# Cross-attention with hand-written order tables: two of three tables rewritten

## The chip, the cores and the metric

The kernel runs on one core of a Trainium2 chip. The metric is the time of one execution on the device in microseconds (us), as the median of several runs. A core has five engines that run side by side: TensorE (PE, matmul; its weight loads are shown as PEld), VectorE (DVE), ScalarE (ACT), GpSimd (POOL) and SyncE (SP), which here does nothing but issue transfers. Each engine works through its own list of instructions in order and waits on semaphores for the others.

## The reference, cut to what matters

The input x is [32, 512, 640], the context is [32, 77, 1024] in the array ctx_2048. The reference takes x as the hidden states and the context's 77 rows as text; only to_q, to_k, to_v and to_out with its bias enter into what the kernel computes:

```python
q = _heads(hidden_states @ to_q_w)          # 20 heads of 32
h_txt = _sdpa(q, _heads(ehs_txt @ to_k_w), _heads(ehs_txt @ to_v_w))
...
out = out @ to_out_w + to_out_b
out = (out + residual) / RESCALE
```

`_sdpa` is the softmax of the scaled scores of 512 queries against 77 keys, times the values, head by head. All is float32.

## The kernel before, in words

**Precision.** Each operand of a matmul is split into a high and a low part, and each product is three matmuls: high by high, high by low, low by high. So most steps below come as "copy the high part" (ACT) and "subtract to get the low part" (DVE or POOL).

**The head.** Lines 300 to 415 compute the keys of all 32 batches, and the values but for the last group of context rows, in five groups of rows, and put them in DRAM (k_dram, v_dram). The split output weights go there too (wo_dram). This takes the first 250 us, and its order isn't part of the tables.

**Slots.** The main part has 160 slots n = 5b + j, one for each batch b and group j of four heads. The steps of a slot are spread over about five slots' time (LAG = 4), so that in any stretch the engines work on several slots. The order in which all of it is issued is written out by hand as a list of tokens, and five engines each take their instructions from it in that order. A token is a letter for the batch (a this one, b the next one), the digit j, a letter for the step, and arguments. `issue` (line 822) turns a token into a call. With n = 5b + j the steps are:

- q0 to q4: three matmuls each, the queries of slot n+1 into one PSUM bank (line 481); Q: its high copy on ACT (715); g0, g1: the low halves on DVE (723); k0, k1: copies to the other partitions on POOL (719).
- s0 to s3: a score tile, three matmuls into one of three PSUM banks (516); m: its negated maximum on DVE (527); e: four exps with sums on ACT (541) into one of two probability buffers pn.
- r, N, z: of slot n-1, the reciprocal (DVE, 551), the scaling (POOL, 556), the transpose (DVE, 562) into the single tile z; w0 to w3: z to DRAM (571). An exp tile of slot n overwrites the pn that z of slot n-2 has read.
- d0, d1: of slot n-3, the rows back from DRAM into raw (586, 588).
- c1, c0, R, l: of slot n-4, the high parts (ACT, 601 and 599) and low parts (DVE 610, POOL 617); v0 to v5: its value passes, one matmul each, into the PSUM tile pa (632); A: half of pa copied to SBUF (ACT, 646); a0, a1: the halves added (DVE, 650).
- h, L: of slot n-5, the high and low part of the attention output at (662, 667); the single pa is free behind L.
- p: three matmuls of the output projection (685); f: the sum with the residual (700); o: its store (703); b: the bias added on POOL (678).
- T, X, x: the transposed and split x of the next batch (278, 288, 292); K: a copy of half of a key tile kb (458).
- u with k, v, x, r: loads of keys (451), values (470), x (274) and residual (674), all on SP.

Tokens with Y (`special`, line 900) are the start: the queries of slot 0 (Yq, YQ, Yg, Yc), and the values of the last group of context rows, whose product with the weights is spread over 40 tokens YC (column group, then the eighth of the sum; three matmuls each, line 191), turned (YT, DVE 228), split (YH on ACT 234, YL on DVE 238) and stored in four parts (YD, issued by POOL, 243). Yk, Yx and Yb load keys, x and bias; Yw0 to Yw4 load the five parts of the output weights from wo_dram (934), into memory that the value weights of columns 0 to 2 held. Ym clears the value tiles. Tokens with Z (`final`, line 936) finish the last batch.

**The tables.** FILL (line 733) holds batches 0 and 1 and the first two score tiles of batch 2, PLAN (771) one batch, run 29 times, and LAST_ (790) the last batch and the end. No scheduler moves anything: what stands earlier in a table is issued earlier on its engine.

```python
    run(0, FILL)
    for b in range(2, B - 1):
        for token in PLAN:
            issue(b, token)
    run(B - 1, LAST_)
```

Of the kernel before, what the change touches and what calls it, by code (L numbers as in the profile page):

```python
# [1024 lines left out]
```

## Time and profile before

| | us |
|---|---|
| median of 3 runs | 1881.04 |
| lowest, highest | 1878.91, 1881.75 |
| the profiled execution | 1879.29 |
| its span in the trace | 1877.4 |
| PE busy in the span | 1855.3 |
| DVE, ACT, POOL busy | 1559.8, 1527.2, 1301.5 |
| first query matmul of FILL | 250.0 |
| last score tile of FILL over | 368.2 |
| first exp tile of slot 0 | 271.1 |

A page of the profile shows one execution. Times in the trace run from the start of the span. A row of a timeline has start, length, engine, line, operation and tiles (written, then read), the number of instructions merged in it, and in brackets the idle time of the engine before it with what ended that. The row of a window has the length and then, for PE, PEld, DVE, ACT and POOL, the busy time with the number of instructions; then the granted clock of PE as a share of full speed, the mean share of the DMA engines and GB/s. A row of the chain of waits has start, length, engine, tile and line. Matmuls are pipelined and overlap in the timeline; in the chain each row runs to the start of the next.

### The profile page before, as it was taken

The numbers are of one execution on the slowest core, as the hardware profiler recorded it, in microseconds if no ns is written. First come the engines' busy times: TensorE is split into PE (matmuls) and PEld (weight loads), VectorE is DVE, ScalarE is ACT, GpSimd is POOL, SyncE is SP. The second block draws the span as 40 slices with busy tenths as digits, with TensorE's granted clock in tenths as the row PEclk, the third lists the DMA queues.
The fourth block names the chain that finished last, engine by engine and source line by source line (L and its number), as shares of the span: only waits on it lengthen the run. The fifth ranks groups of instructions, "written<-read, shape, count | busy, mean of one in ns | idle before, by whom it ended". The sixth has DMA issues, their size and how long they took to land.

```text
span 1877.4 us, 37471 instructions
## 1 busy us (share of the span) xinstructions
PE 1855.3 (99%) x10332; PEld 1662.2 (89%) x10332; DVE 1559.8 (83%) x2494; ACT 1527.2 (81%) x6210; POOL 1301.5 (69%) x1116
## 2 busy tenths in 40 slices
PE   9999998899999999999999999999999999999998
PEld 7888897799999999989999999989999999999988
DVE  5445346999999999999999999989999999999986
ACT  3233237999999999999999999999999999999984
POOL 1100057887788777787877788777887778777874
PEclk9999998999999999999999999999999999999999
DMA  9879869898999998999998998999989999999976
GB/s 190 193 196 251 195 165 249 213 247 239 237 234 237 236 238 226 247 241 232 243 238 231 244 239 236 237 228 247 238 238 242 237 237 239 230 241 236 227 213 205
DMA packets 565022, 431.36 MB, mean 230 GB/s; under 512 B 191120, under 2 KB 473168, under 8 KB 564816
## 3 DMA queue, kind: packets, MB, share of 16 engines
q1 hardware_dynamic: 559760, 413.62, 86.4%
q0 software_dynamic: 4416, 14.34, 2.2%
q8 instruction: 85, 1.39, 0.3%
q14 instruction: 121, 0.99, 0.2%
q10 hardware_dynamic: 640, 1.02, 0.2%
HBM read 247.17 MB, written 181.64 MB: 228 GB/s over the span
## 4 chain that ended last, share of the span: by engine, by line
PE 88%; ACT 3%; DMA 3%; DVE 2%; SPq 2%; issue 1%; POOL 0%; DVEq 0%; ACTq 0%; POOLq 0%
PE po L685 27%; PE pq L481 27%; PE pa L632 11%; PE sc L516 10%; PE pv L191 6%; PE pk L191 6%; ACT pn L541 1%; DMA raw<-pd 1%; DMA xs<-in_x_dram 1%; SPq L571 1%; DMA pd<-z 1%; DMA k_dram<-ks 1%; DVE z L562 0%; DVE pa L650 0%; ACT xt L288 0%
## 5 line engine op out<-in xcount | busy, mean ns | idle before, releaser
L541 ACT ACTIVATE pn<-sc,nm 128x77 f32<-128x77 f32 x2560 | 796.7, 342 | 42.6 <-DVE nm L527 33.1
L685 PE MATMUL po<-wo_s,at 128*128 128x320 f32 x3840 | 710.6, 311 | 0.6 <-DVE xr L700 0.2
L685 PEld LDWEIGHTS po<-wo_s,at 128*128 128x128 f32 x3840 | 620.5, 188 | 43.4 <-DVE xr L700 0.9
L481 PE MATMUL pq<-xt,wq_s 128*128 128x512 f32 x2400 | 600.6, 396 | 2.5 <-DVE qt L723 2.5
L541 ACT ACTIVATION_READ_ACCUMULATOR pn<-sc,nm 128x1 f32 x2560 | 566.9, 222 | 0.0
L481 PEld LDWEIGHTS pq<-xt,wq_s 128*128 128x128 f32 x2400 | 438.2, 189 | 84.7 <-issue 1.9
L556 POOL TENSOR_TENSOR pn<-pn,rs 128x1232 f32<-128x1232 f32 x160 | 389.1, 2432 | 92.7 <-DVE rs L551 89.0
L632 PE MATMUL pa<-pp,vb 128*128 128x512 f32 x960 | 343.3, 406 | 5.4 <-DVE at L667 4.4
L516 PEld LDWEIGHTS sc<-kb,qt 128*128 128x128 f32 x1920 | 305.2, 189 | 22.7 <-ACT pn L541 4.3
L527 DVE TENSOR_REDUCE nm<-sc 128x4 f32<-128x308 f32 x640 | 294.6, 465 | 23.0 <-PE sc L516 17.8
L516 PE MATMUL sc<-kb,qt 128*128 128x154 f32 (+1 forms) x1920 | 304.2, 275 | 6.9 <-ACT pn L541 2.7
L719 POOL CAST qt<-qt 64x512 fp32r<-64x512 f32 x320 | 196.5, 614 | 131.9 <-ACT qt L715 116.8
L650 DVE TENSOR_TENSOR pa<-pa,aw 64x512 f32<-64x512 f32 x320 | 222.3, 695 | 55.7 <-ACT aw L646 48.4
L617 POOL TENSOR_TENSOR pp<-raw,pp 64x512 fp32r<-64x512 f32 x160 | 208.7, 1305 | 77.4 <-ACT pp L599 69.4
L562 DVE STREAM_TRANSPOSE z<-pn 128x1280 f32<-128x1280 f32 x160 | 241.1, 1507 | 6.6 <-DMA pd<-z 2.3
L646 ACT COPY aw<-pa 64x1024 f32<-64x1024 f32 x160 | 162.0, 1012 | 88.8 <-PE pa L632 87.9
L292 POOL TENSOR_TENSOR xt<-xs,xt 128x512 fp32r<-128x512 f32 x160 | 203.2, 1297 | 36.6 <-ACT xt L288 31.5
L723 DVE TENSOR_TENSOR qt<-pq,qt 64x512 fp32r<-64x512 f32 x320 | 216.6, 677 | 13.6 <-ACT qt L715 8.8
L678 POOL TENSOR_TENSOR xr<-xr,bias 128x640 f32<-128x640 f32 x128 | 202.0, 1579 | 14.3 <-DMA xr<-in_x_dram 5.3
L610 DVE TENSOR_TENSOR pp<-raw,pp 128x1024 fp32r<-128x1024 f32 x160 | 194.9, 1218 | 1.2 <-ACT pp L601 1.2
L632 PEld LDWEIGHTS pa<-pp,vb 128*128 128x128 f32 x960 | 174.6, 190 | 17.0 <-issue 4.1
L601 ACT CAST pp<-raw 128x1024 fp32r<-128x1024 f32 x160 | 168.0, 1050 | 0.0
(48 smaller groups left out, 1577.8 us busy)
## 6 DMA issues: line engine op xcount, KB each, us to landing
pd<-z SPq DMA_DIRECT2D x640, 160.0 KB, 3.5
raw<-pd SPq DMA_DIRECT2D x160, 512.0 KB, 4.5
xs<-in_x_dram SPq DMA_DIRECT2D x128, 320.0 KB, 5.7
xr<-in_x_dram SPq DMA_DIRECT2D x128, 320.0 KB, 3.7
out_dram<-xr SPq DMA_DIRECT2D x127, 320.0 KB, 3.7
raw<-pd SPq DMA_DIRECT2D x160, 128.0 KB, 4.1
v_dram<-vs SPq DMA_DIRECT2D x80, 192.0 KB, 4.1
k_dram<-ks POOLq DMA_DIRECT2D x20, 512.0 KB, 4.5
```

The costliest lines, as they stand in the source:

```text
L191: nc.tensor.matmul(held[j][:, :gn], w[:, k, a, :], cts[g, k][:, c, :gn], start=(k == 0 and n == 0), stop=(k == NK - 1 and n == 2),)
L481: nc.tensor.matmul(pqs[n], wq_s[:, k, a, j * P : (j + 1) * P], xts[b, k][:, c, :], start=(k == 0 and m == 0), stop=(k == NC_ - 1 and m == 2),)
L516: nc.tensor.matmul(sc[:, cols], qt[:, m, t * P : (t + 1) * P], keys_, start=(m == 0), stop=(m == 2),)
L527: nc.vector.tensor_reduce(nm, sc[:, :KCOLS].rearrange("p (h k) -> p h k", k=NKEY), AX.X, ALU.max, negate=True)
L541: nc.scalar.activation(pnb[n % 2][:, at, :NKEY], sc[:, i * NKEY : (i + 1) * NKEY], AF.Exp, bias=nm[:, i : i + 1], accum_out=sms[n][:, at : ...
L556: nc.gpsimd.tensor_tensor(pf, pf, rs.unsqueeze(2).to_broadcast([P, NQ * HPC, NKEY]), ALU.mult)
L562: nc.vector.transpose(z.rearrange("p b t j -> p t b j"), pn.rearrange("p (t h) k -> p t (h k)", t=NQ).rearrange("p t (b i) -> p t b i", i=Q),)
L617: nc.gpsimd.tensor_tensor(pp[64:, 4, :], raw[:64, 2, :], pp[:64, 4, :].bitcast(F32), ALU.subtract)
L632: nc.tensor.matmul(pas[n][:, p, :], vb[:, p, t, :], pp[:, c, :], start=(c == p), stop=(c == p + 2),)
L650: nc.vector.tensor_tensor(pa[64 * p : 64 * p + 64, 0], pa[:64, p], aw[:, p], ALU.add)
L685: nc.tensor.matmul(pos[b, t, h][:, :HALF], ats[b * NC_ + j][:, a, t * P : (t + 1) * P], wos[0][:, j, c, h * HALF : (h + 1) * HALF], start= ...
L723: nc.vector.tensor_tensor(qt[rows, 1 + w, :], pqs[n][rows], qt[rows, 0, :].bitcast(F32), ALU.subtract)
```

## The change

The tokens of FILL and of LAST_ stand in another order. Each table has the same tokens as before, 633 in FILL and 468 in LAST_, each once; the functions behind them, PLAN and all the rest of the kernel are the same. In words: the tokens YC of the columns 2 and up stand later among the first queries and scores; the first score tile of slot 0 stands behind 13 of them and not 20; of slot 1, a1s0 and a1s1 stand a little sooner and a1s2 and a1s3 later among the matmuls; Yw0 to Yw4 stand elsewhere; and nearly every other token has another place too, mostly by a few. The core of the diff, with the places that the prediction speaks of:

```diff
     FILL = (
-        "Yq0 YC00 YC10 Yk110 YC11 Yk100 Yq1 Yk000 YC01 Yk101 Ym0 YC12 Yk031 Yk121 YC20 Yk011 YC02 a2uv03 "
-        "Yq2 Yk030 Yk020 Yq3 Yx2 Yq4 Yk010 YC13 Yx1 YQ YC03 Yk120 Yg1 YC04 Yk130 Yg0 Yx0 YC14 a0K01 "
-        "Yk131 YC05 a1K10 a2uv06 a0q0 Yc1 YC06 Ym1 Yk001 a0q1 Yx3 a0q2 Yk111 YC07 b1uv13 a0q3 YT0 Yk021 "
-        "a0q4 a2uv01 YH0 a2uv02 YC15 YL0 a0Q a2uv05 YC30 YD01 Yb a0g0 YC21 a0K00 a2uv07 a0g1 YC31 YD02 "
-        "YC16 Yc0 YC17 YD00 a0s0 YT1 a0s1 YD03 a0m0 YC22 YH1 a1T2 a0e0 a0s2 a0k0 a1q0 a2T3 a0k1 a1q1 "
-        "a0m1 a1T1 a1q2 a0e1 a1q3 YL1 a0m2 YD10 a0s3 a0e2 a1q4 a0m3 YD12 a0T0 YC23 YD11 a1Q a1s0 a0e3 "
-        "YC24 a1k0 a1m0 a1g0 YC25 YD13 a2X0 YC26 a1r a1g1 a1N a1e0 YC27 a1s1 Yw1 YT2 a1s2 Yw4 a1m1 a2q0 "
...
-        "a3q2 a2uv04 YT3 a3x3 b1uv11 a3q3 YH3 a2w0 a3X4 a3q4 YL3 b1uv17 b1uv12 a3s0 a3Q YD32 YC45 "
-        "a3uk000 a3m0 YD31 a3g0 YC46 a3e0 YC47 YD30 a3s1 a3x4 a3d1 YT4 a3s2 a3uk021 a3g1 YH4 YD33 YL4 "
-        "a4q0 a3m1 YD42 a3m2 a3e1 a3s3 a3r YD41 a4q1 a3m3 YD40 a4q2 a3e3 YD43 a4q3 a3k0 a3e2 a4q4 a3k1 "
-        "a4s0 a4Q a3N a4s1 a4g1 a3d0 a4g0 a4d0 a4r a4m0 b0q0 a4N a3z b0q1 a3w1 a4m1 a4e0 a4s2 a3w2 a4k1 "
-        "a4m2 a3w0 a4c1 a4K01 a4s3 a3w3 a4c0 b0q2 b1ur0 a4R a4e1 a4d1 a4l a4v1 b0q3 b1uv10 a4m3 b0q4 "
-        "b0uk100 a4e2 a3uk031 a4v0 a4v2 b0Q a4v4 b0d0 a4z a4v3 a4ux0 a4v5 b0k1 a4A b0uk130 a4k0 b0g1 "
-        "a4w2 b0c0 a4K00 b0uk110 a4a0 a4e3 a4w3 b0k0 b0s0 b0g0 b0d1 b0s1 b0l b0c1 a4w0 a4a1 b1q0 b0m0 "
-        "b0h Yw2 b0m1 b0e0 b0s2 b0L b0r a4ux1 b0R b0N b0v0 b0e1 a4w1 b0v1 a4ux2 b0m2 b0v2 b0ux3 b0v4 "
...
-        "b2uv00 b1a1 b1K11 b1e2 b1uv14 b1K10 b1m3 b1uv15 b2b0 b1a0 b3p0 b2uv04 b1e3 b2m0 b2s1 Yw3 b1z "
-        "b0uk121 b3p1 b2l b2c1 b2q1 b1T1 b1w0 b2h b2q2 b1w2 b2e0 b2m1 b2q3 b0uk101 b1T2 b1w3 b2q4 b2e1 "
-        "b2r b2uv07 b2R b2N b2s2 b1w1 b3p4 b2X0 b0uk111 b2L b2s3 b2X1 b2d0 b2m2 b2v1 b3uk031 b2Q b2m3 "
...
-        "b3k1 b3w0 b4s0 b3m2 b3uk011 b4c0 b3x2 b3a0 b4q0 b4c1 b2uv05 b3a1 b3p7 b4d0 b3x3 b4q1 b3uk021 "
-        "b3m3 b4h b4ur2 b3e3 b4q2 b4L b3uk020 b4l b4p9 b4m0 b3w3 b4p8 b3e2 b4s1 b4f00 b3x4 b4q3 b4f01 "
-        "b4e0 b4r b4s2 b4o0 b4m1 b4v0 b4K00 b4R b3uk030 b4v2 b4q4 b4e1 b4ux2 b4ux1 b4v1 b4m2 b4s3 b4ux0 "
-        "b4Q b4v3 b4N b4m3 b4p10 b4e2 b4g0 b4p15 b4v4 b4p11 b4g1 b4e3 b4v5 b4p12 b4b1 b4z b4p13 b4p14 "
-        "b4A b4w0 b4k1 b4a0 b4w2 b4k0 b4a1 b4w3 b4K01 b4w1 b5d0 b5d1 b5q0 b5c1 b5q1 b5c0 b5q2 b5R b5h "
-        "b5l b5q3 b5uk130 b5q4 b5L b5s0 b5Q b5s1 b5m0 "
+        "YC00 Yq0 YC10 Yk121 Yq1 Yq2 Yk030 Yq3 Yk020 Yk011 Yq4 Ym1 Yk000 YC01 Yk110 YQ YC02 Yk010 a0K01 "
+        "Yg0 Yk120 YC03 Ym0 Yk001 Yg1 YC04 Yk100 YC11 Yk031 a0q0 Yc0 Yk130 a2uv03 a0q1 a2uv05 YC05 Yk111 "
+        "a1K10 a0q2 b1uv17 a1K11 Yk021 YC12 Yc1 Yx1 YC13 Yx0 a0K00 YC14 Yx3 a0q3 Yx2 YC06 a2uv04 Yb YC15 "
+        "a2uv02 a0q4 b1uv14 a0s0 a0Q YC07 b1uv11 a0g1 a0k0 YC20 YC16 a0g0 a0k1 Yk101 YC17 YT0 a0s1 a0m0 "
+        "YH0 YC21 a0m1 a2uv07 a0e0 YT1 a1q0 YL0 YC22 a0e1 a0T0 YD00 a0s2 YC23 YD02 a0m2 YH1 a1q1 YD03 "
+        "a0e2 YL1 a0s3 YD01 a1q2 a0m3 a2T3 a1s0 a0e3 YD10 a1q3 a1T1 YD13 a1q4 a1m0 YD11 YC24 a1Q YC25 "
+        "a1g0 a1k0 YC26 a1r YD12 a1s1 a1g1 YC27 a1N YC30 Yw0 YT2 YC31 Yw1 a1T2 YH2 a2uv01 YC32 a1m1 a2X0 "
...
+        "a3q4 a3x2 a2w3 YC42 a3Q a2w1 YC43 a2e2 a3x3 a3g0 a2w2 YC44 a2w0 a3g1 YC45 a2e1 YD32 a3uk020 "
+        "YC46 a3uk000 YD33 YC47 a3uk010 a3x4 a4q0 YT4 a3s0 YH4 a3s1 a2e3 YL4 a4q1 a3m0 YD43 a4q2 a3m1 "
+        "a3e0 YD41 a4q3 YD40 a3s2 a3e1 a4q4 YD42 a3m2 a3r a3s3 a3N a4Q a3m3 a3e2 a4g0 a4g1 a3e3 a3d0 "
+        "a3d1 a3z b0q0 a4K01 b1uv13 a3k0 b0q1 a4k0 b0q2 a3w1 a3w3 a4k1 a4d0 a3k1 a4s0 a3w0 a4c1 a4K00 "
+        "a4s1 a3w2 a4m0 b0q3 a4m1 a4c0 a4d1 a4R a4s2 a4e0 a4ux0 a4l b0q4 b0ux3 a4m2 a4e1 a4r a4s3 a4v0 "
+        "b0uk130 a4m3 a4v2 b0Q a4v4 a4e2 b0s0 b0k0 a4v1 b0m0 a4v3 a4v5 b0g0 a4N b0d0 a4A b0g1 b0uk121 "
+        "b0c0 a4ux2 a4a1 b1q0 a4ux1 a4e3 a4a0 b0s1 b0d1 b0l b1q1 a4z b0h b0s2 b0c1 b0k1 b1q2 b0L a4w3 "
...
+        "b1uv12 b1m3 b3p4 b2c0 b0uk131 b1a0 b2q1 b1e3 b1uv10 b2l b1a1 b2uv02 b2q2 b2m0 b2q3 b1e2 b2d0 "
+        "b1T2 b1K11 b2uv06 b2q4 b1K10 b1z b2uv00 b2h b2b0 b3p5 b2d1 b2c1 b2s1 b2L b3p2 b1w3 b2e0 b2m1 "
+        "b1w2 b2R b2v0 b1w1 b2Q b2v1 b2s2 b2e1 b1w0 b2s3 b2k0 b2m2 b2v2 b2uv05 b2m3 b2v3 b2v5 b2k1 b2r "
+        "b3uk000 b3p6 b2e2 b2g0 b2uv03 b2N b2g1 Yw3 b2e3 b3uk020 b3s0 b2T3 b3uk030 b3s1 b3ur1 b2v4 b2X0 "
...
+        "b3m3 b3p7 b3X4 b3z b3x2 b3uk001 b4s0 b3A b4q0 b3uk021 b3x3 b4q1 b4c0 b3a0 b4d0 b3e3 b3w1 b4q2 "
+        "b3a1 b3x4 b3w2 b4q3 b4h b3w0 b4s1 b4c1 b3w3 b4L b4q4 b4l b4ux2 b4m0 b4p8 b3e2 b4m1 b4ur2 b4p9 "
+        "b4R b4K00 b4v0 b4v2 b4Q b4v1 b4s2 b4e0 b4f00 b4v3 b4v4 b4g0 b4v5 b4k0 b4p10 b4f01 b4A b4p11 "
+        "b4k1 b4o0 b4g1 b4p12 b4ux1 b4K01 b5c1 b4s3 b4r b5d1 b4m2 b5q0 b4N b4m3 b4ux0 b5c0 b5q1 b4a1 "
+        "b4e2 b4p13 b4a0 b5q2 b5h b4z b5q3 b5l b4e1 b5s0 b5q4 b4b1 b5R b4e3 b4w1 b4p15 b4w0 b4p14 b4w3 "
+        "b5L b5s1 b5Q b4w2 b5m0 b5uk130 b5d0 "
     ).split()
```

```diff
     LAST_ = (
...
-        "a4p10 a4m1 a4A a4N a4s2 b0d0 a4p11 a4ur2 a4m2 a4p12 a4e0 a4a0 b0d1 a4p13 a4a1 a4p14 b0c0 a4p15 "
-        "b0f10 b0c1 b0p16 b0l a4z b0p17 b0p20 b0h a4s3 a4e1 b0p21 a4w1 a4m3 b0p18 b0L a4w3 a4e3 b0p19 "
...
-        "b1p31 b1c0 b0z b2p35 b1c1 b1l Zp00 Zp10 b1L Zp20 b0w0 b2p36 b1R b0w2 b1v1 b1v3 b0w3 b1b3 b1v0 "
-        "b1v2 b0w1 b1v4 b1v5 Zp30 b1ur0 b1A b2p32 b1uv16 Zp21 b2c0 b1a1 b2p33 b2c1 b2p34 b2l b1a0 b2d0 "
-        "b2p37 b2d1 b2f30 b2p38 b2h b2o2 Zp11 b2L b2p39 b2R Zp01 b2v0 b2v2 b2v1 b3f31 b2v3 b2v4 b3o3 "
-        "b2v5 Zp40 b2A Zp50 Zp12 b3c0 b2a1 Zp51 b3ur1 b3c1 Zp41 b3l b2a0 Zp42 Zp22 b3h Zp52 b3L Zp31 b3R "
-        "b3v1 b3v0 Zx b3v3 b4b1 b3v2 b3v5 b3v4 Zp32 b3A Zp23 Zp43 b3a0 Zp02 Zp13 b3a1 b4ur2 Zb3 Zp53 "
-        "Zp33 b4h Zp03 b4L Zp04 b2b0 Zp60 Zp34 Zp24 Zb2 Zp61 Zp14 Zp62 Zf01 Zp54 Zf00 Zp63 Zf10 Zo0 Zp64 "
-        "Zf11 Zp70 Zo1 Zf30 Zp44 Zo30 Zp71 Zf20 Zp72 Zf21 Zp73 Zo2 Zp74 Zf31 Zo31 "
...
+        "b0d0 a4s2 a4m1 a4p10 b1uv14 a4e0 a4a1 a4p11 b0d1 a4p12 a4a0 b0b2 a4p15 a4z b0p16 b0h b0p17 b0c1 "
+        "a4s3 a4p13 b0c0 a4w3 a4m2 a4p14 b0L a4e1 a4w0 b0p18 b0l b0f10 b0p19 a4w2 a4m3 b0v1 a4o0 b0f11 "
...
+        "b1c1 b2o2 b0z b2p32 b2p35 Zp00 b1L Zp10 b0w3 b2p36 b0w1 b1R b1v1 b1b3 b0w2 b1v0 b1v2 b1v3 b0w0 "
+        "b1v5 b1v4 b1ur0 b2p33 b1A b1uv12 Zp20 Zp11 b1uv16 b2c0 b1a0 Zp30 b2c1 b2p34 b2l b2d0 b1a1 b2p37 "
+        "b2d1 b2f30 b2p38 b2h b3ur1 Zp40 b2L b2p39 b2R b2v1 b2v0 b2v3 b2v2 b3f31 b2v4 b2v5 Zp50 b2A Zp41 "
+        "Zp21 b3c0 b2a0 Zp31 b3c1 Zx Zp51 b3l b2a1 Zp22 b3o3 Zp52 b3h Zp42 b3L Zp32 b3R b3v0 b3v1 b3v2 "
+        "b3v3 Zb3 b3v5 b3v4 Zp23 b4ur2 b3A Zp43 Zp53 b4b1 b3a1 Zp12 Zp01 b3a0 Zp33 b2b0 Zp02 b4h Zp03 "
+        "b4L Zp13 Zb2 Zp24 Zp14 Zp04 Zp34 Zp60 Zf11 Zp61 Zf10 Zp62 Zf01 Zp63 Zf00 Zp70 Zo0 Zp44 Zo1 Zp64 "
+        "Zp54 Zf30 Zp71 Zf20 Zo30 Zp72 Zf21 Zp73 Zo2 Zp74 Zf31 Zo31 "
     ).split()
```

56 rows, old and new, of tables (FILL, LAST_) are left out of this document.

## The prediction

> **What bounds the kernel now.** I read the busy time by stage first, cut at the ends of the tables.
>
> ```profile
> 294.42:318.77 24.35, 18.98 (x82) 15.34 (x80) 15.23 (x26) 16.69 (x74) 18.70 (x21) 0.86 0.91 244
> 318.77:368.20 49.43, 42.71 (x208) 34.53 (x209) 42.90 (x64) 45.27 (x191) 36.94 (x29) 0.97 0.88 221
> 368.20:1795.70 1427.50, 1426.87 (x8267) 1295.15 (x8266) 1303.04 (x2090) 1314.97 (x5510) 1140.87 (x958) 1.00 0.92 238
> 1795.70:1877.40 81.70, 76.74 (x466) 70.48 (x464) 59.90 (x97) 52.67 (x197) 46.57 (x34) 0.99 0.67 200
> ```
>
> The columns are length, then busy time of PE, PEld, DVE, ACT and POOL, then the granted PE clock. From 368.20 to 1795.70 PE works 1426.87 of 1427.50 us: that is PLAN, whose table is unchanged, so nothing can be won there, and a time that FILL gains or loses reaches the end undiminished while PE stays full. Left are FILL, from 250.0 to 368.2, and LAST_. In the last 74 us of FILL, PE idles 5.37 and then 6.72 us, and the mean clock is below 1.
>
> What FILL must cost comes from the chain of waits, where matmuls stand without overlap:
>
> ```profile
> 271.82 2.78 PE pq L481 x12
> ...
> 282.61 0.32 PE sc L516 x3
> ...
> 287.13 2.87 PE pv L191 x15
> ...
> 389.07 2.24 PE po L685 x15
> ...
> 391.98 0.47 PE pa L632 x2
> ```
>
> A query token (3 matmuls) is 2.78/4 = 0.695 us, a context-value token 2.87/5 = 0.574, a score tile 0.33, a value pass 0.235, a projection 2.24/5 = 0.448. FILL has 60, 40, 42, 36 and 16 of them in either table: 41.7 + 23.0 + 13.9 + 8.5 + 7.2 = 94.3 us. It takes 118.2 (from 250.02, below, to 368.20), so 23.9 us are lost there, and that is the ceiling of any gain.
>
> ```profile
> 250.02 0.86 PE L481 MATMUL pq<-xt,wq_s 128*128 128x512 f32 x3
> ...
> 270.20 0.68 PE L516 MATMUL sc<-kb,qt 128*128 128x154 f32 x4 [1.45 <-DMA vb<-v_dram]
> ```
>
> **The change part by part.** Each table holds the same tokens as before; no instruction is added or removed. So I take the places where PE waits, and lay the new order out from there with these durations.
>
> *First scores (a0s0).* Before, ten query and 20 context tokens stand ahead: 6.95 + 11.48 = 18.4, PE arrives at 268.4 and waits 1.45 us. The wait is put down to a vb load, but the score needs kb:
>
> ```profile
> 252.98 3.35 SPq L451 DMA_DIRECT2D kb<-k_dram  x7
> 258.88 0.30 SPq L470 DMA_DIRECT2D vb<-v_dram  x1
> ...
> 266.67 0.42 SPq L451 DMA_DIRECT2D kb<-k_dram  x1
> ```
>
> SP issues seven key loads at 0.48 each, then is held until 258.88 by a value load; the last key load of that group (Yk021) goes out at 266.67 to 267.09, and the score restarts 3.1 us behind it, at 270.20. In the new table 12 key loads precede the first value load (252.98 + 12 x 0.48 = 258.7), and Yk021 is the fifth issue from 258.88: out at about 261, its data there by 264.1; the four x loads now stand behind it. PE now has 13 context tokens ahead of a0s0: 6.95 + 7.46 = 14.4, so it would arrive at 264.4. But Yq0 to Yq4 are over earlier, and the next query, a0q0, waits for both low halves of slot 0:
>
> ```profile
> 255.72 0.54 ACTq L213 DMA_DIRECT2D k_dram<-ks  x1
> 257.64 0.59 ACT L715 CAST qt<-pq 128x512 fp32r<-128x512 f32 x1 [2.58 <-PE pq L481]
> ```
>
> ```profile
> 258.26 1.39 DVE L723 TENSOR_TENSOR qt<-pq,qt 64x512 fp32r<-64x512 f32 x2 [2.58 <-ACT qt L715]
> ```
>
> ACT is held by the key store until 255.72 + 0.54 = 256.26, then copies (0.59), then DVE subtracts (1.39): 258.25, where PE comes at 250.02 + 5 x 0.695 + 7 x 0.574 = 257.5. So 1.45 us goes and 0.8 to 0.9 comes; a0s0 starts at 265.3, three us sooner. The tiles of the second slot: a1s0 moves from about 24 to 22 us of PE work behind the start, a1s2 and a1s3 move the other way (27 to 29 and 28 to 31). That lead isn't kept: the copy YH2 now stands ahead of a1e0 on ACT and needs the last context token of its column, so by a2e0 I find ACT where it was, within 1 us. PE, without a wait, reaches a3s0 at 295.9 (before at 294.42, the cut of the rows above), having done three more context tokens and one more query, 2.4 us of work: 0.9 ahead. Cost of all this so far: nothing to one us gained.
>
> *The hand-over (a3s0 to a4A), where before loses most.*
>
> ```profile
> 294.75 1.90 PE L191 MATMUL pv<-ct,wv_s 128*128 128x416 f32 x9
> ```
>
> ```profile
> 298.95 2.55 POOL L243 DMA_DIRECT2D v_dram<-vs  x4 [0.28 <-DVE vs L238]
> 301.55 1.27 POOL L719 CAST qt<-qt 64x512 fp32r<-64x512 f32 x2
> 302.91 4.56 POOL L556 TENSOR_TENSOR pn<-pn,rs 128x1232 f32<-128x1232 f32 x2
> ```
>
> ```profile
> 305.31 1.49 DVE L562 STREAM_TRANSPOSE z<-pn 128x1280 f32<-128x1280 f32 x1
> ```
>
> ```profile
> 306.91 0.33 ACT L541 ACTIVATE pn<-sc,nm 128x77 f32<-128x77 f32 x1 [3.44 <-DVE z L562]
> ...
> 314.59 1.01 ACT L646 COPY aw<-pa 64x1024 f32<-64x1024 f32 x1 [0.57 <-PE pa L632]
> ```
>
> ```profile
> L541 ACT ACTIVATE pn<-sc,nm 128x77 f32<-128x77 f32 x2560 | 796.7, 342 | 42.6 <-DVE nm L527 33.1
> ```
>
> Before, the last context tokens end at 294.75 + 1.90 = 296.65; 2.3 us later, behind a transpose, a copy and a subtraction of these, POOL starts four value stores (to 301.5), then two query copies (1.27), then a3N (half of 4.56 = 2.28), then comes a3z (to 306.8), and only then may a4e0 overwrite the same probabilities: ACT waits 3.44 us, to 306.91. The new table puts the query copies behind a3N. Its context tokens end at 250.02 + 0.9 + 44.3 = 295.2 (ahead of that stand 40 of them, 25 queries and 12 score tiles: 23.0 + 17.4 + 3.9); 2.3 later the stores start, to 300.05; a3N ends at 302.3. DVE has the two subtractions of a4Q ahead of a3z; a4Q follows a3e1, the third exp tile behind the copy YH4 (295.2 + about 1.2 + 3.7 = 300.2), so these end there too (0.6 + 1.39: 302.2), and a3z at 303.8, three us sooner than before. PE pays: b0q0 waits for the same subtractions from 300.0 to 302.3, and a4s0 for the copy a3k1, now the fifth cast behind a3N (302.3 + 5 x 0.62 = 305.4, by the 1.27 for two). Then come a4s0 (0.33), its maximum (about 0.45) and on ACT a4e0, a4e1, b0Q and a4e2 at 1.245 an exp tile (796.7/640) and 0.6 for b0Q, the casts a4c1 and a4c0 being done before: a4A starts at 310.6 against 314.59, 4.0 sooner.
>
> From this I take back the half clock:
>
> ```profile
> 302.76:306.17 3.41, 1.84 (x9) 1.55 (x10) 2.65 (x5) 0.71 (x3) 3.29 (x3) 1.00 0.89 320
> 306.17:313.00 6.83, 6.07 (x19) 4.79 (x18) 4.14 (x6) 5.22 (x26) 4.28 (x4) 0.50 0.71 177
> 313.00:316.41 3.41, 1.95 (x10) 1.34 (x9) 1.89 (x4) 2.38 (x5) 2.16 (x4) 1.00 1.03 247
> 316.41:319.83 3.42, 1.89 (x13) 1.52 (x11) 2.97 (x7) 3.42 (x17) 1.47 (x2) 1.00 1.15 277
> 319.83:323.24 3.41, 3.41 (x10) 2.74 (x11) 1.42 (x2) 2.06 (x12) 3.03 (x1) 0.50 1.02 284
> ```
>
> Twice (306.17 and 319.83) the clock falls to 0.50 behind a window with PE busy 1.84 or 1.89 of 3.41; a third window with 1.95 stays at 1.00, and after a window full of matmuls it is back. In the new order the window 299.35 to 302.76 has PE busy 0.65 + 0.45 = 1.1 us, less than either. So I expect half speed from 302.76: the query matmuls left there (2.1 - 0.45 = 1.6) take 3.2, a4s0 comes at 306.0, and a4A starts at 311.3: **3.3 us ahead**. [...]
>
> *From a4A to the end of FILL.* From 314.59 to 329.12 (b1e0) ACT is busy 12.61 us and idle 1.92; then it has 36.81 in 39.01:
>
> ```profile
> 314.59:329.12 14.53, 10.71 (x43) 8.21 (x43) 10.62 (x18) 12.61 (x49) 8.42 (x9) 0.88 1.01 256
> 329.12:368.13 39.01, 34.15 (x177) 28.08 (x178) 35.19 (x53) 36.81 (x155) 31.57 (x26) 1.00 0.86 217
> ```
>
> ACT is the bound of this part, and either table leaves it the same tokens behind b1e0. In the new order b0A waits for its value passes (0.8) and little else, so 1.3 idle against 1.92: 0.6 more. In the tail b4Q moves ahead of b4e0 and waits for b4q4, which stands behind a score tile whose bank b3e2 frees: 0.33 + 0.70 + 0.1, and b4A waits about 1: 2.1, against the 2.2 before. Zero. The output weights keep wide cover but for Yw3, which now goes out behind b1w0 and the key load b3uk000, for which SP waits until b2s3 is read (I place it at 333, its first projection at 341, so 8 us for one load); Yw0, Yw1 and Yw4 wait on SP for the context tokens of columns 0 to 2, as before, and hold only loads that are due 10 us later. If a raw row were late, ACT would wait at a c token, and that is no more than the bound that follows. Bounds for the tail: 2.2 gained, if all its idle went, to 2.3 lost, if the new waits came on top of the old.
>
> *LAST_.* PE idles 81.70 - 76.74 = 4.96, most of it behind its last matmul.
>
> ```profile
> 1860.60 1.77 PE L632 MATMUL pa<-pp,vb 128*128 128x512 f32 x6 [0.81 <-DVE at L667]
> ```
>
> The wait of 0.81 ends the chain from the last scores through their transpose z and its way out to DRAM and back. a4s3 stands three projections earlier (1.3 us), so that chain may start up to 1 us sooner; but between the passes of b1v and of b2v stand nine projections instead of ten, 0.45 less cover for the same chain of copy, additions and subtraction. I take 0.3 gained, between 0.8 gained and 0.8 lost.
>
> Sum: 3.3 + 0.6 + 0 + 0.3 = **4.2 us**. The profiled execution took 1879.29 (span 1877.4 and 1.9 around it), so 1875.1 for such a one; the median of the three runs stands 1.75 above it, 1881.04, so I predict **1876.8**.
>
> **The rivals.**
> 1. *No half clock in the new order* (17%). For it: the window with 1.95 stayed at 1.00. Against: 1.1 is far below. Then 4.0 + 0.6 + 0.3 and 0.9 more, as the second window, at 319.83, goes too: 5.8, so 1875.2. [...]
> 2. *The lead is given back in the tail* (20%): the new ACT waits for b4q4, for b4A's passes, and for b2q4 (b2Q now ahead of b2e1) come on top of the 2.2 us that were idle. For it: ACT is 94% busy there, so a wait isn't made up. Against: the waits of before fall at the same tokens. 4.2 less 2.3 to 4: about 1880.
> 3. *Slower, by the clock* (15%). PE waits longer at a time in the new order (2.3, 0.7, then 2.1 and 0.8 at the score banks of b1s0 and b1s1). Each window at 0.50 costs up to 1.7 us where ACT waits for PE. Before has three such windows; with five more (8.5) against the 4.2 won it is 4.3 slower: 1885.3. It decides from three more. Against: one full window restored the clock each time.
> 4. That "sooner scores" isn't what the table does is half true already (a1s2 and a1s3 go later); it is in the sum.
>
> **How the numbers follow.** Forecast 48%, with a range of its own from 1875 to 1879; rivals 17, 20 and 15. About 0.2% (3.8 us) is what a measurement of this kernel can tell from no change, so faster means below 1877.28 and slower above 1884.8. The forecast stands just inside: 0.29 of its 0.48, rival 1 whole and 0.02 of rival 2 make faster 0.48; rival 3 is slower, 0.15; the rest is same, 0.37. The range goes from 1873.2 (rival 1 and 2 us of the tail's idle) to 1882.0 (rival 2 with LAST_ at its worse end); it leaves out rival 3 and a little below.
>
> **What would show it.** Right: the first wait of a score for vb or kb gone and a short wait of a0q0 for qt near 257.5; a3N on POOL before 300.5; a4A near 311; clock 0.50 once from about 302.8; PE full from about 364; PLAN's 1427 us unchanged. Wrong: a4A at or behind 313, more than three windows at 0.50, ACT idle over 4 us between b1e0 and the end of FILL, or a PE wait over 1 us in LAST_.

## The result and the profile after

The changed kernel takes **1874.24 us** (median of 10 runs, 1872.94 to 1876.58), the kernel before on the same chip 1878.78 (10 runs, 1875.72 to 1881.75). The ratio is 0.9976, with a 95% interval from 0.9966 to 0.9985: 4.5 us faster (2.8 to 6.4), where the forecast was 4.2. The time itself was forecast at 1876.8, 2.6 us too high: that started from 1881.04, the median of three runs of the kernel before, and ten runs put it at 1878.78. So 1874.24 lies just outside the forecast's narrow range (1875 to 1879) and inside the wide one.

The profiled execution of the changed kernel took 1872.94 us (span 1871.1, mean clock 0.997). The two profiles differ by 6.3 us and the medians by 4.5, so part of what they show is the scatter of single executions.

The view by stage, with the columns of the prediction and cut at a0s0, a3s0, b0e0 and the end of FILL (the last cut stands about 0.6 us ahead of the end of PLAN, 1789.1):

```profile
265.57:296.90 31.33, 31.26 (x166) 28.58 (x165) 21.69 (x37) 20.76 (x101) 24.17 (x29) 1.00 0.95 248
296.90:315.90 19.00, 14.99 (x77) 11.80 (x76) 13.84 (x23) 17.17 (x82) 15.19 (x17) 1.00 0.90 233
315.90:362.92 47.02, 42.00 (x203) 34.31 (x202) 42.41 (x66) 44.70 (x191) 36.26 (x29) 0.93 0.92 243
362.92:1788.54 1425.62, 1425.62 (x8263) 1294.47 (x8262) 1301.91 (x2088) 1313.72 (x5511) 1137.71 (x958) 1.00 0.92 238
1788.54:1871.10 82.56, 77.25 (x470) 71.13 (x469) 61.08 (x98) 52.71 (x198) 47.72 (x35) 1.00 0.66 199
```

FILL ends at 362.92 for 368.20. From 250.0 on PE idles 10.2 us for 13.5 and is busy 102.7 for 104.7, so of the 5.28 us 3.3 are idle time; the other 2.0 are in line with 3.4 us less at half clock. PLAN is full, as before. LAST_ keeps about 5 us of idle time, as before. The clock is whole up to b0e0 (0.86 before) and lower behind it (0.93 for 0.97).

Matching each token of the tables to its instruction gives the lead over before at the points that the prediction laid out:

| token | before | after | difference | forecast |
|---|---|---|---|---|
| a0s0, first score tile | 268.26 | 265.57 | -2.69 | 265.3 |
| a2e0, third exp slot | 284.17 | 287.63 | +3.46 | within 1 |
| a3s0 | 294.42 | 296.90 | +2.48 | 295.9 |
| a3N, normalization | 302.91 | 301.13 | -1.78 | ends 302.3 |
| a3z, transpose | 305.31 | 303.44 | -1.87 | ends 303.8 |
| a4A | 314.59 | 311.71 | -2.88 | 311.3 |
| b1e0 | 329.13 | 325.36 | -3.77 | -3.9 |
| end of FILL | 368.20 | 362.92 | -5.28 | -3.9 |
| last transfer issued | 1874.31 | 1867.66 | -6.65 | -4.2 |

Between the end of FILL and that of PLAN the lead grows by another 1.3 us. Of this, 0.8 are two steps of 0.4 in PLAN, which is the same in both kernels; first_new below, whose time is that of before, gains the same two steps on the profiled execution of before. They belong to that execution, not to the change.

ScalarE's waits are the short form of the story, since it is the bound from the hand-over to the end of FILL. Columns: engine, line, who was waited for, us in total, times, longest. Before, from 295 to the end of FILL:

```profile
ACT pn L541 <- DVE z L562: 3.4, 1, 3.4
ACT pn L541 <- DVE nm L527: 2.8, 3, 1.3
ACT aw L646 <- PE pa L632: 1.9, 2, 1.4
ACT qt L715 <- PE pq L481: 1.7, 2, 1.3
ACT at L662 <- DVE pa L650: 1.4, 2, 0.8
```

After, over the same part:

```profile
ACT aw L646 <- PE pa L632: 2.1, 3, 1.0
ACT vs L234 <- ACT pn L541: 1.0, 1, 1.0
ACT pp L601 <- DMA v_dram<-vs: 0.8, 1, 0.8
ACT pn L541 <- DVE nm L527: 0.8, 1, 0.8
```

The wait for the transpose z is gone, as forecast. Two of the three waits for a maximum (nm) and both for an addition (pa) are gone too, and little of this was in the sum.

The granted clock, on the windows in which it changes in the new kernel's execution:

```profile
298.50:301.91 3.41, 2.78 (x16) 2.23 (x14) 1.70 (x6) 3.41 (x22) 3.34 (x5) 1.00 0.81 181
301.91:305.33 3.42, 1.97 (x9) 1.65 (x10) 2.80 (x3) 2.62 (x17) 3.26 (x5) 1.00 0.65 229
...
318.99:322.40 3.41, 1.31 (x7) 0.67 (x5) 2.92 (x5) 3.38 (x12) 1.43 (x1) 1.00 0.98 239
322.40:325.81 3.41, 2.71 (x8) 1.99 (x9) 3.41 (x6) 3.41 (x21) 1.52 (x2) 0.50 0.93 307
325.81:329.23 3.42, 3.42 (x13) 3.03 (x13) 2.66 (x5) 2.62 (x15) 3.23 (x3) 0.50 1.00 258
329.23:332.64 3.41, 3.41 (x19) 2.93 (x19) 3.27 (x6) 3.38 (x18) 2.13 (x3) 1.00 0.58 160
```

The half clock that I expected from 302.76 didn't come; one came at 322.40, behind a window with PE busy 1.31. These windows begin 0.84 us off those of before, and that matters below.

### The profile page after: what moved, and what is told of

Its sections match the earlier page's. It is cut to its first block, busy times and chain, and to the rows that moved or that the text cites. A ratio compares the mean times of both kernels' runs of the same rounds, so it can differ in the third digit from the quotient of the medians.

```text
span 1871.1 us, 37477 instructions
## 1 busy us (share of the span) xinstructions
PE 1852.1 (99%) x10332; PEld 1660.1 (89%) x10332; DVE 1559.3 (83%) x2494; ACT 1525.0 (82%) x6210; POOL 1298.7 (69%) x1116
## 4 chain that ended last, share of the span: by engine, by line
PE 81%; ACT 1%; DVE 1%; DMA 1%; issue 0%; POOL 0%; SPq 0%; DVEq 0%; POOLq 0%; ACTq 0%
PE po L685 30%; PE pq L481 28%; PE pa L632 12%; PE sc L516 11%; ACT pn L541 1%; DMA pd<-z 0%; DMA raw<-pd 0%; DVE qt L723 0%; ACT pp L601 0%; DVE z L562 0%; SPq L571 0%; DVE xs L278 0%; POOL v_dram L243 0%; PE pv L191 0%; DVE nm L527 0%
## 5 line engine op out<-in xcount | busy, mean ns | idle before, releaser
L556 POOL TENSOR_TENSOR pn<-pn,rs 128x1232 f32<-128x1232 f32 x160 | 387.0, 2419 | 88.9 <-DVE rs L551 87.0
L516 PEld LDWEIGHTS sc<-kb,qt 128*128 128x128 f32 x1920 | 305.4, 189 | 20.7 <-ACT pn L541 6.1
L527 DVE TENSOR_REDUCE nm<-sc 128x4 f32<-128x308 f32 x640 | 294.9, 466 | 22.8 <-PE sc L516 17.1
L610 DVE TENSOR_TENSOR pp<-raw,pp 128x1024 fp32r<-128x1024 f32 x160 | 194.3, 1214 | 0.0
```

The source lines that it names most:

```text
L516: nc.tensor.matmul(sc[:, cols], qt[:, m, t * P : (t + 1) * P], keys_, start=(m == 0), stop=(m == 2),)
L527: nc.vector.tensor_reduce(nm, sc[:, :KCOLS].rearrange("p (h k) -> p h k", k=NKEY), AX.X, ALU.max, negate=True)
L556: nc.gpsimd.tensor_tensor(pf, pf, rs.unsqueeze(2).to_broadcast([P, NQ * HPC, NKEY]), ALU.mult)
```

## The experiments

Each kernel ran 11 times, the kernel before 33 times beside it (medians 1878.73, 1878.12 and 1877.70 for the three groups of four). "Hand-over" is the time from the start of YC47, the last context token, to b1e0; "tail" from there to the start of b5s1, the last score tile. Both leave out what the 295 us ahead scatter: with one and the same opening order YC47 starts anywhere from 294.0 to 296.1.

| kernel | ratio to before (95%) | half clock, 290 to 370 | hand-over | tail | b4R |
|---|---|---|---|---|---|
| before | | 10.2 | 33.2 | 38.5 | 3.19 |
| last_new | 1.0001 (0.9992 to 1.0010) | 10.2 | 33.0 | 39.8 | 3.19 |
| first_new | 1.0002 (0.9993 to 1.0011) | 6.8 | 32.6 | 39.7 | 4.91 |
| query_later | 1.0005 (0.9995 to 1.0016) | 17.1 | 33.9 | 38.7 | 3.19 |
| before_warm | 1.0017 (1.0008 to 1.0026) | 6.8 | 35.1 | 38.7 | 3.19 |
| to_a4A | 1.0014 (1.0005 to 1.0023) | 17.1 | 34.0 | 39.6 | 3.19 |
| rest_first | 0.9990 (0.9981 to 0.9998) | 3.4 | 31.5 | 37.6 | 1.21 |
| to_b1e0 | 0.9996 (0.9987 to 1.0005) | 13.7 | 30.1 | 39.5 | 3.19 |
| after | 0.9976 (0.9966 to 0.9985) | 6.8 | 29.7 | 37.1 | 1.44 |
| fill_new | 0.9977 (0.9969 to 0.9986) | 6.8 | 30.1 | 36.8 | 1.43 |
| rest_new | 0.9989 (0.9980 to 0.9998) | 6.8 | 30.8 | 36.6 | 1.41 |
| query_first | 0.9985 (0.9976 to 0.9994) | 10.2 | 31.5 | 37.1 | 1.43 |
| after_warm | 0.9984 (0.9975 to 0.9992) | 3.4 | 31.5 | 36.2 | 1.44 |
| exp_first | 0.9985 (0.9976 to 0.9993) | 6.8 | 30.4 | 37.1 | 1.43 |

The last four columns are us of the one profiled execution. The theory on record says: the hand-over gives 3.3, the way from a4A to b1e0 0.6, the tail nothing, LAST_ 0.3. A second theory grew from the two traces: the old tail loses time of its own, by b4R.

**fill_new** and **last_new**: one table each.

```diff
-    FILL = ( "Yq0 YC00 YC10 Yk110 YC11 Yk100 Yq1
+    FILL = ( "YC00 Yq0 YC10 Yk121 Yq1 Yq2 Yk030
```

> FILL is the new table, LAST_ the old one. My theory: FILL carries nearly all of the change, because PE stays full through PLAN; the two profiles put FILL's end 5.28 us earlier and 5.8 by the second batch of PLAN, against 4.5 between the medians. So 4.0 to 5.0 us faster than the kernel before. Rival, that LAST_ carries a share: then 3 us or less here.

```diff
-    LAST_ = ( "a0p16 a0f10 a0ur3 a0r a0N
+    LAST_ = ( "a0r a1d0 a0v1 a0e0 a0m1
```

> FILL is the old table, LAST_ the new one. My theory: between 0 and 0.5 us faster (I forecast 0.3; the two profiles show 0.1 between the start of LAST_ and the last transfer). Rival, that LAST_ carries a share: over 1 us faster.

Measured: 0.9977 (4.3 us faster) and 1.0001. FILL carries the change whole; LAST_ is worth nothing that can be measured, and 0.3 can't be told from it.

**first_new** and **rest_new**: the opening of FILL new with the rest old, and the reverse.

```diff
 first_new: new order up to YC47, then the old
+... YC46 a3uk000 YD33 YC47 b1uv13 b1uv16 a3uk010 a2e3 b1uv12 a3s0 a3m0 a3e0 ...
 rest_new: old order up to YC47, then the new
+... YC46 a3e0 YC47 b1uv14 a3uk021 a3uk031 YD30 b1uv15 a3g1 YD33 a3x4 a4q0 ...
```

> The tokens that the new table has up to YC47 (the last context token) stand in their new order, all others behind them in the old order. This tests the forecast that the earlier first scores are worth 0 to 1 us by the end: the wait of 1.45 us at a0s0 goes, PE has 2.4 us more of context and query work done at YC47, and the hand-over is as before. My theory: FILL ends within 1 us of before (368.20), the time is 0 to 1 us less. Rival, that the lead of the first scores reaches the end: 2 us or more faster.

> The reverse: the old order up to YC47, then all that is left in the new order. My theory: the gain is made at and behind the hand-over, so 3 to 5 us faster, with a3z before 305.5 and a4A before 313. Rival, that the new opening is what makes the hand-over earlier: a4A stays near 314.6 and the time within 1 us of before.

Measured: 1.0002, and 0.9989, about 2 us faster (0.4 to 3.8). The opening alone is worth nothing, as forecast, though a0s0 starts 2.70 us earlier. What follows is worth something by itself, but by the times less than the 3 to 5 expected. In its profiled execution FILL ends 5.00 us earlier than before, as in fill_new (5.04), so the two differ in LAST_, where they have the same table. This ScalarE row of rest_new is a copy of LAST_ (b0c0) that waits for the last rows on their way back from DRAM:

```profile
1833.11 0.62 ACT L599 CAST pp<-raw 64x512 fp32r<-64x512 f32 x1 [2.24 <-DMA raw<-pd]
```

The same copy before:

```profile
1837.35 0.62 ACT L599 CAST pp<-raw 64x512 fp32r<-64x512 f32 x1 [0.46 <-DMA raw<-pd]
```

With one and the same LAST_ this wait differs by 1.8 us between two executions, and ScalarE's lead over before falls there from 6.0 to 4.25 us. It explains the profiled execution, not the median, so why rest_new's median lies behind fill_new's (some 2 us by the ratios) stays open; the intervals of the two overlap.

**to_a4A**: the new order up to a4A, then the old.

```diff
+... b0g0 a4N b0d0 a4A b1uv16 b1uv12 b1ur0 b1uv10 b0uk100 a4z b0k1 b0g1 a4w2 ...
```

> New order up to a4A, then the old order for all that is left. My recorded theory: the tail is worth nothing in either order, so this ends like the new kernel, 4 to 4.5 us faster than before. Rival, from the two traces: the old tail loses about 2 us of its own, because b4R (VectorE, raw minus its high part) stands in the trace with 3.19 us for 1.21 when b4N on GpSimd starts 0.17 us ahead of it, and b4e2 on ScalarE then waits 1.22 us for a maximum; then b4R is over 2.5 us long here too, and this is 2 to 3 us faster only.

Both missed: 1.0014, 2.6 us slower. The lead is there at a4A (312.48, 2.1 ahead) and nearly gone at b0e0 (318.40 for 318.77). The seam did it. These are VectorE's rows (start, length, engine, line, what it does, idle before it and for whom):

```profile
312.19 0.67 DVE L723 TENSOR_TENSOR qt<-pq,qt 64x512 fp32r<-64x512 f32 x1
314.19 1.51 DVE L562 STREAM_TRANSPOSE z<-pn 128x1280 f32<-128x1280 f32 x1 [1.32 <-POOL pn L556]
315.74 0.69 DVE L723 TENSOR_TENSOR qt<-pq,qt 64x512 fp32r<-64x512 f32 x1
```

And TensorE's:

```profile
316.49 1.65 PE L481 MATMUL pq<-xt,wq_s 128*128 128x512 f32 x3 [3.46 <-DVE qt L723]
```

The old order has a4z ahead of the second subtraction b0g1; behind the new hand-over a4z waits for a4N, b0g1 stands behind it, and b1q0 waits 3.46 us for the bank that b0g1 empties. It isn't a fair price of the tail, but it shows that the hand-over's lead isn't kept by itself: what comes next on VectorE must be laid for it. b4R was 3.19 us long, as the second theory says.

**to_b1e0**: the same cut at b1e0, with no such turn.

```diff
+... b1Q b0w3 b1s2 b1e0 b1uv12 b1ur0 b1uv10 b1v3 b1k1 b1v5 b1k0 b1g0 b1m1 b1r ...
```

> New order up to b1e0, old order behind it. It cuts the gain at a place where no token of VectorE is turned about across the seam (at a4A the old a4z came ahead of b0g1 and TensorE waited 3.46 us). Theory of two causes: b1e0 3 to 4 us earlier, then b4R again 3 us long beside b4N, and the tail gives back 1.5 to 2: FILL ends 1.5 to 3 us earlier than before, the time 1 to 3 us less. Rival, my recorded one, that the tail is worth nothing: the time is that of the new kernel, 4 to 4.5 us less than before.

Measured: 0.9996, between 2.4 us faster and 0.9 slower; the hand-over takes 30.1 us, like the new kernel, and the tail 39.5, like the old. By these stretches **the tail is worth about as much as the hand-over**, and my recorded "zero" falls. The time, 0.8 us less, lies just under the 1 to 3 that the theory of two causes gave, and leaves the tail the larger part; the interval is too wide to split the gain by it.

**rest_first**: one token of the old tail moved.

```diff
-... b4f01 b4e0 b4r b4s2 b4o0 b4m1 b4v0 b4K00 b4R b3uk030 ...
+... b4f01 b4e0 b4s2 b4o0 b4m1 b4v0 b4K00 b4R b4r b3uk030 ...
```

> The old kernel with one token moved: b4r (the reciprocal that b4N waits for) goes behind b4m1 and b4R on VectorE, so b4R starts ahead of b4N. [...]

Two readings of the 3.19 us of b4R can be told apart here: that it is long because b4N runs beside it, or by its data, which the move doesn't change. VectorE before, with b4R (L610) as the long row:

```profile
357.82 0.25 DVE L551 RECIPROCAL rs<-sm 128x16 f32<-128x16 f32 x1
357.99 0.41 DVE L527 TENSOR_REDUCE nm<-sc 128x4 f32<-128x308 f32 x1
358.32 3.19 DVE L610 TENSOR_TENSOR pp<-raw,pp 128x1024 fp32r<-128x1024 f32 x1
361.43 0.85 DVE L527 TENSOR_REDUCE nm<-sc 128x4 f32<-128x308 f32 x2
```

GpSimd before, at the same time:

```profile
358.15 2.28 POOL L556 TENSOR_TENSOR pn<-pn,rs 128x1232 f32<-128x1232 f32 x1 [0.38 <-DVE rs L551]
360.38 2.54 POOL L678 TENSOR_TENSOR xr<-xr,bias 128x640 f32<-128x640 f32 x1
```

VectorE in rest_first:

```profile
354.94 0.47 DVE L527 TENSOR_REDUCE nm<-sc 128x4 f32<-128x308 f32 x1
355.32 1.21 DVE L610 TENSOR_TENSOR pp<-raw,pp 128x1024 fp32r<-128x1024 f32 x1
356.45 0.24 DVE L551 RECIPROCAL rs<-sm 128x16 f32<-128x16 f32 x1
```

And GpSimd there:

```profile
356.78 2.28 POOL L556 TENSOR_TENSOR pn<-pn,rs 128x1232 f32<-128x1232 f32 x1 [1.39 <-DVE rs L551]
359.01 1.59 POOL L678 TENSOR_TENSOR xr<-xr,bias 128x640 f32<-128x640 f32 x1
```

Before, b4r ends, b4N starts on GpSimd at 358.15, and b4R starts 0.17 us behind it. b4R ends at 361.51: that is 1.08 behind the end of b4N (360.43), nearly its whole length of 1.21 once more. In its turn the bias addition (2.54 for 1.59) ends at 362.92, 1.41 behind the end of b4R. No wait is shown for either; only the length tells. With b4r behind b4R all three have their normal lengths. The time is 0.9990, about 1.9 us less (0.4 to 3.6), and the tail 37.6 for 38.5 (39.5 behind the new hand-over). So b4R was long by b4N beside it and not by its data. The price of that is about the 1 us that the tail is shorter: the rest of what this execution gained up to the end of FILL (3.4 us in all) lies ahead of the moved token, where the clock was at half for 3.4 us and not 10.2. The interval of the time holds 1 us as well as 1.9.

**query_later** and **query_first**: the query copies alone, in the old and in the new kernel.

```diff
 query_later, in the old order
-... a4q3 a3k0 a3e2 a4q4 a3k1 a4s0 a4Q a3N a4s1 a4g1 ...
+... a4q3 a3e2 a4q4 a4Q a3N a3k0 a3k1 a4s0 a4s1 a4g1 ...
 query_first, in the new order
-... a3s3 a3N a4Q a3m3 ... a4K01 b1uv13 a3k0 b0q1 ... a4d0 a3k1 a4s0 ...
+... a3s3 a3k0 a3k1 a3N a4Q a3m3 ... a4K01 b1uv13 b0q1 ... a4d0 a4s0 ...
```

> The old kernel with one move: the query copies a3k0 and a3k1 and the score tile a4s0 that needs them go behind a3N. My recorded theory takes this as the heart of the gain at the hand-over: a3N 1.27 us earlier. But VectorE still does the two subtractions of a4Q (to 304.9) ahead of a3z, as a4Q isn't moved: so a3z at 304.9 for 305.31, a4s0 at 305.1, and a4A 0.3 to 1 us earlier, the time 0 to 0.7 us less. Rival, that the place of the query copies alone makes the hand-over: a3z 1.3 earlier and 2 us or more at a4A.

> The new kernel with the query copies a3k0 and a3k1 put back ahead of a3N, all else as in the new kernel. Theory: a3N and a3z 1.2 to 1.3 us later (a3z at 304.7), the way of these rows out and back shifts by as much, a4A at 312.5 to 313 and FILL's end 0.8 to 1.3 us later: half to one and a half us slower than the new kernel, 3 to 4 us faster than the kernel before. Rival, that ScalarE waits for a4s0 rather than for the rows: then a4s0 comes earlier, and nothing is lost.

Measured: 1.0005 and 0.9985. In the old order a3N starts 2.0 us earlier, and a3z at 305.34 for 305.31: VectorE has a4Q's subtractions ahead of it, as expected (to 304.3), and then a4m0, the maximum of the a4s0 that was moved too, for which it waits 0.53 us; so nothing is won. a4A is 1.7 earlier all the same (312.93), as in last_new with the old FILL unchanged (312.79), and at b0e0 the lead is gone (318.71 for 318.77). In the new order a3z is 1.0 later (304.45), the hand-over 1.3 to 1.7 us longer than in after and fill_new, in line with the expectation, though 0.9985 and 0.9976 can't be told apart by their intervals. So by these stretches the place of the copies is worth something in the new order, where a4Q stands ahead of a3e2 and a3e3, and nothing in the old. What a4Q's own place is worth wasn't tested.

**before_warm** and **after_warm**: matmuls in PE's gaps, to keep the clock whole.

```diff
+        for _ in range(int(token[4])):   # again(token): the three matmuls of score_tile
+                nc.tensor.matmul(sc[:, cols], qt[:, m, t * P : (t + 1) * P], keys_, start=(m == 0), stop=(m == 2))
 before_warm
+... a4s1 Wa414 ...   ... a4v5 Wa433 ...   ... b0s2 Wb023 ...
 after_warm
+... a3m3 Wa332 ...   ... a4v5 Wb003 ...   ... b1q4 Wb035 ...
```

> The old kernel with score tiles computed again, to the same values, where TensorE waits in the hand-over: a4s1 four times more behind itself, a4s3 three times behind a4v5, b0s2 three times behind itself (30 matmuls of work added, nothing left out). It tests the price of the half clock. The half clock of before (10.2 us of it between 306 and 323) should go. Theory that it is a real part of the old loss: a4A to b1e0 come 1.5 to 2 us earlier, and the time is 1 to 2 us less. Rival, that the waits for ScalarE and the rows cover it: under 0.5 us, or slower by what the added matmuls hold up.

> The new kernel with the same kind of filling: a3s3 twice more behind a3m3, b0s0 three times behind a4v5, b1s0's wait filled with b0s3 five times behind b1q4 (30 matmuls added, nothing left out). The new order lost one or two stretches at half clock, 6.8 us in all. Theory: the clock stays whole, and 0.3 to 1 us is won, so this is the fastest version. Rival: ScalarE is the bound there and nothing is won, or the added matmuls delay b0q0 or b1s0 and cost up to 1 us.

before_warm failed as an experiment: 1.0017. The three repeats of a4s3 stand behind the key load b0uk100, which replaces some of the keys that they read (so these repeats don't have the same values, as I had written). They waited for it, and b0s0 behind them for a key copy that waited for the repeats:

```profile
PE sc L516 <- POOL kb L458: 2.1, 1, 2.1
PE sc L981 <- DMA kb<-k_dram: 1.2, 1, 1.2
```

Up to a4A, ahead of that mishap, the clock was whole, and a4A came 2.1 us sooner (312.48). In last_new and rest_first, which have the old order there unchanged, the half clock also fell behind a4A. Counted from the start of YC47, a4A comes after 16.9 us in all three and after 18.7 in before, so the half clock costs the old order 1.7 us at a4A. How much of that is left at b1e0 the scatter among unchanged hand-overs shows: 31.5 with 3.4 us at half clock (rest_first), 33.0 with 6.8 (last_new, whose third stretch lies in the tail) and 33.2 with 10.2 (before).

after_warm filled the gap at 319.7, and the clock there stayed whole (1.00 from 318.0 to 324.8). Its tail is the shortest of all, by 0.4 to 0.9 us. But the filler behind a3m3 didn't keep the clock from falling at 303.12, and it held up VectorE's subtractions of a4Q, as the rival had it for the added matmuls:

```profile
301.34 1.41 DVE L723 TENSOR_TENSOR qt<-pq,qt 64x512 fp32r<-64x512 f32 x2 [1.07 <-PE sc L981]
```

The hand-over is 31.5. By the time it is 0.9984, the same as after within the intervals, so it isn't the fastest version, and filling the gaps in this way wins nothing that can be measured. It doesn't price the half clock in the hand-over, which it didn't remove.

**exp_first**: one token of the new opening.

```diff
-... YT2 YC31 Yw1 a1T2 YH2 ... a1z Yw4 a1k1 a1e0 a2q1 ...
+... YT2 YC31 Yw1 a1T2 a1e0 YH2 ... a1z Yw4 a1k1 a2q1 ...
```

> The new kernel with one token moved: a1e0, the first exp tile of the second slot, goes ahead of the copy YH2 on ScalarE. My recorded step says that the new table loses the lead of the first scores there (a1e0 2.8 us later than before), and that ScalarE has the time to make it up. Theory: a1e0 3 to 5 us earlier, a2e0 within 1 us and FILL's end within 0.5 us of the new kernel's. Rival, that YH2 now comes late: the last context stores and a3N go later by 1 us or more, and the time with them.

Measured: a1e0 at 277.65 (280.84 in after), a2e0 at 287.52 (287.63), the time 0.9985. The lead of 3.2 us is gone one slot later. FILL's end came 0.9 behind after's and 0.7 behind fill_new's, a little more than expected; a cause for that wasn't sought.

No version beat the new kernel: 0.9976 and 0.9977 (fill_new, which is the new kernel but for the worthless LAST_) are the lowest ratios.

## Why the prediction was right, point by point

The sum was right (4.2 forecast, 4.5 measured) with two terms that missed in opposite directions: the end of the context tokens, 1.45 us ahead in the sum and 0.3 in the pair of profiles, and the tail, worth nothing in the sum and about 2.4 us in the runs. That the two nearly cancel is luck.

- *First scores: nothing to 1 us.* Right. The wait for the keys went, and a0q0 waited from 257.53 for 1.11 us (0.8 to 0.9 forecast; the times laid out there give 0.75). first_new prices it at zero. One thing was laid out wrong: a2e0 came 3.5 us later than before, not "within 1", and nobody missed it, as ScalarE had the time.
- *Hand-over: a4A 3.3 ahead.* a4A came at 311.71 (311.3 forecast), by the chain laid out: the stores, a3N, the query copies behind it, a3k1 as the fifth cast, a4s0, a4e0. But two misses cancelled. The context tokens ended 1.2 us later than worked out (296.36 for 295.2), so a3N ended at 303.41 for 302.3; by the test that I gave (a3N starting before 300.5) this step failed. The sum of durations runs short: for the old order (25 queries, 13 score tiles and 40 context tokens from 250.02, and the wait of 1.45) it gives 296.1, where 296.65 was measured, so setting the sum for the new order beside a measured end made 0.6 of the lead. And the half clock, for which I took 0.7, didn't come in that execution.
- *The half clock from 302.76.* This is the step that was wrong in kind. I read the busy time of the new order on the window grid of the old execution. The new executions had other grids: half windows begin at 306.17 before, at 322.40 after, and in fill_new, with the same FILL as after, at 304.56 (17.84 us ahead of after's, 5.2 windows of 3.41). In fill_new, rest_new, query_first, to_b1e0, after_warm and to_a4A it did fall in the hand-over of the new order, between 303.1 and 305.4, and not in after and exp_first. The windows of fill_new:

```profile
301.15:304.56 3.41, 1.32 (x8) 1.03 (x7) 2.82 (x4) 3.25 (x19) 3.28 (x4) 1.00 0.80 285
304.56:307.98 3.42, 3.42 (x13) 2.94 (x12) 1.00 (x2) 1.62 (x3) 3.24 (x6) 0.50 0.55 107
307.98:311.39 3.41, 3.41 (x21) 2.97 (x21) 2.66 (x6) 3.41 (x21) 0.96 (x2) 1.00 1.02 313
```

  The wait of PE behind a3s3 is as long there (2.09 us) as in after (2.08), but lies within one window (1.32 busy), where in after it is cut in two (2.78 and 1.97). FILL ended within 0.3 us in after and fill_new all the same. Counted from the start of YC47, a4A comes after 16.1 and 16.5 us in after and exp_first, and after 16.4 to 16.5 in fill_new, to_a4A and to_b1e0: where the half clock comes, it costs the new order at most 0.4 us at a4A, and not 0.7.
- *a4A to b1e0: 0.6.* 0.9 in the pair of profiles (2.88 to 3.77). Over several executions the hand-over up to b1e0 takes 31.5 to 33.9 us in the old order (before, last_new, first_new, query_later, rest_first) and 29.7 to 30.8 in the new (after, fill_new, rest_new, to_b1e0, exp_first): means of 32.8 and 30.2, so about 2.6 us. Of the 3.9 forecast for b1e0, 1.45 was laid to the context tokens' earlier end, which leaves 2.45 for this stretch: its size came true. The part ahead of it didn't: YC47 starts at 295.5 in the mean of six executions with the old opening and at 295.4 in that of eight with the new.
- *Tail: 0.* **The mis-sized term.** 36.2 to 37.1 us in six kernels with the new tail, 38.5 to 39.8 in seven with the old one and a long b4R: means of 36.8 and 39.2, 2.4 us. I had counted the 2.2 us that ScalarE waits in the old tail, and put waits of my own in their place: b4Q for b4q4, and b4A for its passes, 2.1. b4Q came without a wait, and b4A waited 0.3 in after. In the six with the new tail ScalarE is idle 0.5 to 1.3 us there, in the seven with the old one 2.2 to 3.4, and in rest_first 1.3. And I hadn't asked why b4R stands with 3.19 us when its line's median is 1.21. rest_first shows b4R to be about 1 us of the tail; the rest, the new order's other moves, wasn't split further.
- *LAST_: 0.3.* last_new lies between 1.5 us faster and 1.9 slower, and the pair of profiles shows 0.1. The forecast can't be told from zero.

The rivals: *no half clock* came true only up to 322.40 in after's execution and 323.01 in exp_first's, where the clock fell for 6.8 us, and not in the others, so it isn't a case of its own but went with where the windows fell (a wait of 2.08 us cut in two by them in after, one of 2.09 within one in fill_new). *Lead given back in the tail* is refuted: the tail adds to it. *Slower by the clock* is refuted by the times, and in the profiles no kernel with the new FILL had more than three half windows, and those with one to three differ by under 1.8 us from YC47 to FILL's end. A lead can be lost in this way, though: to_a4A with a lead of 2.1 at a4A ended 2.6 us slower than before, with one bad wait (3.46) and 17.1 us at half clock for 10.2.

## What to carry to other kernels

Read a row that is far longer than its line's median (b4R, 3.19 us for 1.21) as a wait that no view lists, and look at what VectorE and GpSimd did in the same microsecond. Price a hand-over by what stands next on each engine behind it: moving only the token that was late (query_later) or only the part that was won (to_a4A) gave nothing or less. Where effects are of 2 us, compare stretches between tokens over several executions, since the opening (294.0 to 296.1), the clock (1.7 us at a4A in the old order) and one DMA (a wait of 0.46 or 2.24) each scattered by about 2 us here.
